# Sums rounded by one ScalarE step, statistics moved to ScalarE, and a copy moved on by one element, in a binary-convolution network

## The chip, the cores and the metric

The kernel runs on one core of a Trainium2 chip. The metric is the device time of one execution in microseconds (us). TensorE is called PE here, VectorE DVE, ScalarE ACT, GpSimd POOL, and SP is the engine that issues most DMAs.

## The reference

Four layers work on `x` of 16 images, 256 channels, 28 x 28 pixels. The change touches layers 0 and 2.

```python
# layer 0: signs convolved with signs, 3 x 3, padding 1, then a norm over batch and pixels
y  = conv3x3(sign(x), sign(w)) * mean(abs(w))      # per output channel
x  = (y - mean(y)) * rsqrt(var(y) + 1e-5) * gamma + beta + x
# layer 1: a convolution with full-precision weights on signs, a 1 x 1 one, gates
...
# layer 2: two convolutions of signs, each followed by prelu; norms before, between and after
out = sign(batchnorm(x, g1, b1))
out = prelu(conv3x3(out, sf1 * sign(w1)), a1)
out = sign(batchnorm(out, g2, b2))
out = prelu(conv3x3(out, sf2 * sign(w2)), a2)
x   = prelu(batchnorm(out, g3, b3) + x, a3)
# layer 3: attention over the 784 pixels
```

A sum over 256 channels and 9 taps of +1, -1 and 0 is a whole number of at most 2304 in size.

## The kernel before, in words

All work of one image is laid out with 128 channels on the partitions and two halves of the channels, `k` of the input and `mo` of the output. A convolution of signs (`sign_layer`) computes both output halves in one matmul: the 16-bit weight of a tap is `PACK * w[mo=1] + w[mo=0]` with `PACK = 4095`, so each PSUM value holds two whole numbers. One matmul (line L353) handles 128 input channels, one tap and half an image, 392 pixels. A **block** is half an image: 2 input halves x 3 rows of taps (`CHUNKS`) x 3 taps of a row = 18 matmuls into one PSUM bank. Layer 2 has two such convolutions of 32 blocks each (`HALVES`); layer 0 has the same 32 halves, of which the first 14 images are handled as whole images and the last half image in two quarters (`whole_images`, `PARTS`).

The moving operand comes from `fpads`, padded sign images of 30 x 30 in 16 bits for two images in turn; a tap of column `c` reads rows of 28 elements that begin `c` elements into the padded row. `sign_image(i + 1)` is issued on ACT (L466 in layer 0, L1172 in layer 2) in the first block of image `i`, ahead of that block's own eviction.

A block leaves PSUM in `apart(j)`. The value divided by `PACK` is rounded to the nearest whole number by two ACT steps: L364 adds 1.5 * 2^23 (`rounding`), L365 subtracts it (`unrounding`), which gives half 1. DVE then takes `PACK` times half 1 from the PSUM value, which gives half 0 (L367). The result lies in `ab`, in layer 2 f32 with three buffers, in layer 0 the 16-bit tile `n`, which POOL stores to `n0d` (L628) and SP loads again in layer 1 (L455).

`post(j - 1)` works on the block before. In layer 0 it takes statistics (L626, BN_STATS). In layer 2, for each half, DVE applies prelu into `p` (L1206) and takes BN_STATS of `p` (L1208); ACT squares half 0 into `doubts` (L1211), a check whether the two numbers were ever too large to be taken apart.

`Moments` keeps the statistics. Parts below `EARLY = 22` go into `parts`, and `gather` reduces them to one entry in the middle of block 23 (L169, L170); the later parts lie beside that entry in `fin`, and after the last block `mom()` reduces `fin` (L186). The next layer's scale and shift, and its first sign, wait for that: this is the seam between two convolutions. PE is kept warm over it by matmuls on zeros (`keep_busy`, L446).

PE, ACT, DVE and SP run `sign_layer` in an order written out by hand (`tc.manual_schedule`). For iteration `j` this is: the matmuls of block `j`; on a first half the sign of the next image; `post(j - 1)` on DVE; at one block `gather`; `apart(j)`; and then the squares of block `j - 1` on ACT. Three PSUM tiles (`conv_ps`) serve the blocks in turn.

SP's loads of `p` for later images of layer 2's first convolution (`load_p`, L1181) are issued within the sign of an earlier one: `load_p(i + 5)` with `sign2a(i)`. L432 are two loads of the same kind for the attention.

Layer 1 (L750) reads its middle taps, from the second image on, from `one_on`, a copy moved on by one element which SP makes (`move_on`, L724).

Of the kernel before, what the change touches and what calls it, by code (L numbers as in the profile page):

```python
# [31 lines left out]
I16 = mybir.dt.int16  # L32
# [51 lines left out]
def forward(ctx: ExitStack, tc: tile.TileContext, d: dict, out: bass.AP, careful: bool):  # L84
# [68 lines left out]
    class Moments:  # L153


        def __init__(self, name, early, late, early_count):
            self.parts = const.tile([P, 2, early, 6], F32, tag="parts", name=name + "_parts")
            self.fin = const.tile([P, 2, 3 + 6 * late], F32, name=name + "_fin")
            self.mv = const.tile([P, 2, 2], F32, name=name + "_mv")
            self.early, self.count, self.name = early, float(early_count), name  # L160

        def part(self, at, k):
            return self.parts[:, k, at, :] if at < self.early else self.fin[:, k, 6 * (at - self.early) + 3:][:, 0:6]

        def gather(self):

            nc.gpsimd.memset(self.fin[:, :, 0:1], self.count)
            for k in range(2):
                V.bn_aggr(self.fin[:, k, 1:3], self.parts[:, k].rearrange("p c s -> p (c s)"))  # L169
            V.tensor_scalar(self.fin[:, :, 2:3], self.fin[:, :, 2:3], self.count, None, ALU.mult)  # L170
# [164 lines left out]
    def sign_layer(pads, w, temp, room, sign, post, steps, moments, blocks, together=1):  # L335
# [9 lines left out]
        def products(*js):  # L345
            for j in js:
                pss[j] = conv_ps()
            for n, (k, g) in enumerate(CHUNKS):
                for j, (h, r0, rows) in ((j, p) for j in js for p in pieces(blocks[j])):
                    for t in range(3):  # L350
                        r, c = divmod(3 * g + t, 3)
                        r += r0
                        T.matmul(  # L353
                            pss[j][:, n // size if careful else h, :rows * S].rearrange("p (a b) -> p a b", b=S),
                            lhsT=w[:, n, t, :], rhs=pads[:, blocks[j][0] % 2, k, r:r + rows, c:c + S],
                            start=(n % size == 0 and t == 0), stop=(n % size == size - 1 and t == 2),
                        )

        def apart(j):
            for g in range(groups):  # L360
                n = blocks[j][2] * S
                t, ab = temp("t1")[:, :n], room(blocks[j], g)
                ps = pss[j][:, :, :HN] if blocks[j][2] == S else pss[j][:, g, :n]
                A.activation(by_halves(t, blocks[j]), ps, AF.Identity, bias=rounding, scale=1.0 / PACK)  # L364
                A.activation(ab[:, 1], t, AF.Identity, bias=unrounding)  # L365
                a, b = (by_halves(ab[:, mo], blocks[j]) for mo in range(2))
                V.scalar_tensor_tensor(a, b, -PACK, ps, ALU.mult, ALU.add)  # L367
                if g == 0:
                    abs_[j] = ab
                else:  # L370
                    tt(abs_[j], abs_[j], ab, ALU.add)

        def sign_image(i):

            for r0, r1 in ((0, HR + 1), (HR + 1, S)) if i == 0 else ((0, S),):
                sign(i, slice(r0, r1), lambda k: inner(pads[:, i % 2], k, r0, r1))
# [39 lines left out]
    def block_moments(name, blocks):  # L416
        return Moments(name, EARLY, len(blocks) - EARLY, EARLY * HN)
# [16 lines left out]
    with tc.tile_pool(name="ps_conv", bufs=3, space=PSUM) as psc, \  # L434
# [13 lines left out]
        with tc.tile_pool(name="ph1", bufs=1) as ph:  # L448
# [15 lines left out]
            def sign0(b, rows, out):  # L464
                for k in range(2):
                    A.activation(out(k), img(xs[b][:, k, :])[:, rows], AF.Sign, saturate=False)  # L466
                if rows.stop == S and b + 3 < B:
                    load_x(b + 3)
# [684 lines left out]
        with tc.tile_pool(name="ph2", bufs=1) as ph:  # L1153
# [8 lines left out]
            def room2(block, part):  # L1162
                return ph.tile([P, 2, HN], F32, tag="ab", name="ab", bufs=3)[:, :, :block[2] * S]
# [19 lines left out]
            def sign2a(i, rows, out):  # L1183
                sign2(x2[order[i]], sg1, bg1, rows, out)
                if rows.stop == S and i + 5 < B:
                    load_p(i + 5)
# [4 lines left out]
            def post2(order, alpha, mom, doubt):  # L1191
# [4 lines left out]
                def post(block, ab):  # L1196
                    i, r0, rows = block
                    for mo in range(2):
# [6 lines left out]
                        else:  # L1205
                            V.scalar_tensor_tensor(p, y, alpha[:, mo:mo + 1], y, ALU.mult, ALU.max)  # L1206
                        for h, _, m in pieces(block):
                            V.bn_stats(mom.part(first_part(block) + h, mo), p[:, h * HN:h * HN + m * S])  # L1208

                    def square(h, m):  # L1210
                        A.activation(  # L1211
                            temp("t2")[:, :m * S], ab[:, 0, h * HN:h * HN + m * S], AF.Square, scale=SAFE**-0.5,
                            accum_out=doubt[:, first_part(block) + h:first_part(block) + h + 1],
                        )

                    squares = [lambda h=h, m=m: square(h, m) for h, _, m in pieces(block) if not careful]
                    if i < B - 1:
# [13 lines left out]
            if careful:  # L1231
# [7 lines left out]
            mom = block_moments("l2b", HALVES)  # L1239
            sign_layer(fpads, w2a, temp, room2, sign2a, post2(order, pv("a1"), mom, doubts[:, 2 * NB:3 * NB]), steps, mom, HALVES)  # L1240
# [5 lines left out]
            mom = block_moments("l2c", HALVES)  # L1246
            sign_layer(
                fpads, w2b, temp, room2, lambda i, rows, out: sign2(pt[i], sg2, bg2, rows, out),
                post2(range(B), pv("a2"), mom, doubts[:, 3 * NB:4 * NB]), [], mom, HALVES,
# [606 lines left out]
```

## Time and profile before

| | |
|---|---|
| time, median of 3 runs | 956.71 us (956.46 to 960.13) |
| profiled execution | 956.87 us, of which the span from first to last instruction is 955.0 us |
| layer 0, first to last L353 | 7 to 108 us of the span |
| layer 2, first convolution | 463.8 to 561.8 us |
| layer 2, second convolution | 568.9 to 667.0 us |
| L353, one matmul as the profile shows it | 329 ns, overlapping the next |
| ACT L364, L365 on half an image | 587, 622 ns |
| DVE L367, L1206, L1208 on half an image | 547, 620, 570 ns |
| granted TensorE clock | 0.997 |

The profile is one profiled execution. Its page gives the busy time of each engine and the chain of work that ended last, followed back from the end: at each step to what released it. The chain can be had in order of time. The timeline lists instructions in order of start, with the idle time of the engine before one and what ended it in brackets; neighbours of one kind are merged (x and a count). A DMA's time to landing runs from its issue to its data's arrival.

### The profile page before, as it was taken

How to read it: one execution, taken by the hardware profiler on the slowest of the kernel's cores; microseconds unless marked ns; L12 is line 12 of the kernel's file. 1: busy time of each engine (PE TensorE's matmuls, PEld its weight loads, DVE VectorE, ACT ScalarE, POOL GpSimd, SP SyncE). 2: the span in 40 equal slices, each digit the busy share in tenths (PEclk: the TensorE clock that was granted, in tenths of full speed). 3: DMA queues.
4: the chain of work that ended last, by engine and by line, in shares of the span. 5: the costliest groups of instructions: out<-in, count | busy, mean ns of one | idle time of the engine just before them, and what ended most of it. 6: DMA issues, size and time to landing. Idle time of an engine off the chain costs nothing.

```text
span 955.0 us, 14909 instructions
## 1 busy us (share of the span) xinstructions
PE 936.3 (98%) x5602; PEld 581.9 (61%) x5608; DVE 772.2 (81%) x1424; ACT 718.9 (75%) x1204; POOL 136.2 (14%) x143
## 2 busy tenths in 40 slices
PE   7999999999999999999999999999999999999996
PEld 3555578787888888787555555555444444444442
DVE  3877898999998899977799978999656868677765
ACT  6887778888887888865788868887766666676652
POOL 2001100000000000000000000000235353434431
PEclk9999999999999999999999999999999999999998
DMA  9887534445533444411670000000142433434212
GB/s 331 277 305 263 181 120 138 167 179 202 185 138 138 156 170 162 148 71 68 250 290 1 1 1 2 1 1 1 26 77 68 98 107 83 120 74 131 68 68 106
DMA packets 35591, 118.73 MB, mean 124 GB/s; under 512 B 4451, under 2 KB 15909, under 8 KB 35509
## 3 DMA queue, kind: packets, MB, share of 16 engines
q1 hardware_dynamic: 29588, 86.33, 25.4%
q0 software_dynamic: 5632, 30.54, 11.9%
q8 instruction: 46, 0.75, 0.3%
q10 hardware_dynamic: 288, 0.80, 0.3%
q14 instruction: 37, 0.30, 0.1%
HBM read 72.67 MB, written 32.11 MB: 110 GB/s over the span
## 4 chain that ended last, share of the span: by engine, by line
PE 84%; DVE 7%; issue 3%; ACT 3%; DMA 2%; SPq 1%; POOL 0%; DVEq 0%; POOLq 0%; ACTq 0%
PE cv L750 29%; PE cv L353 21%; PE sc L1422 8%; PE av L1443 8%; PE cv L877 5%; PE mi L1399 5%; DVE p L1206 2%; PE sm L1485 2%; PE mi L1503 2%; PE sm L1443 1%; DVE ab L367 1%; DMA xs<-in_x_dram 1%; DVE l2c_fin L1208 1%; DVE l2b_fin L1208 1%; PE gate L845 1%
## 5 line engine op out<-in xcount | busy, mean ns | idle before, releaser
L353 PE MATMUL cv<-fpads,wpk 128*128 128x392 f16 (+1 forms) x1746 | 294.9, 331 | 2.7 <-DVE wpk L280 1.3
L750 PE MATMUL cv<-vs,w 128*128 128x392 f32 (+1 forms) x1296 | 272.4, 352 | 1.1 <-DVE vs L134 1.1
L353 PEld LDWEIGHTS <-wpk 128*128 128x128 f16 x1746 | 169.3, 97 | 128.9 <-issue 3.6
L750 PEld LDWEIGHTS cv<-vs,w 128*128 128x128 f32 x768 | 143.2, 190 | 6.2
L1426 ACT ACTIVATE es<-sc 128x784 f32<-128x784 f32 x112 | 87.3, 822 | 41.7 <-PE sc L1422 41.7
L750 PEld LDWEIGHTS <-w 128*128 128x128 f16 x768 | 69.4, 99 | 52.8 <-issue 9.1
L1422 PE MATMUL sc<-q,keyswa 64*128 64x392 f32 x448 | 89.9, 513 | 0.9 <-ACT es L1426 0.9
L364 ACT ACTIVATE t<-cv,rounding 128x392 f32<-128x392 f32 (+2 forms) x83 | 52.1, 628 | 38.7 <-PE cv L353 38.7
L1206 DVE SCALAR_TENSOR_TENSOR p<-ab,vec 128x392 f32<-128x392 f32 x128 | 79.2, 618 | 2.3
L1443 PE MATMUL av<-es,v 128*64 128x392 f32 x448 | 80.7, 499 | 0.0
L1436 POOL TENSOR_TENSOR sum<-sum,es 128x784 f32<-128x784 f32 x32 | 67.2, 2100 | 3.1 <-ACT es L1426 0.6
L1422 PEld LDWEIGHTS sc<-q,keyswa 64*128 64x128 f32 x448 | 38.9, 186 | 44.0 <-issue 17.1
L750 PE MATMUL cv<-one_on,w 128*128 128x392 bf16 x240 | 59.4, 329 | 0.0
L1410 DVE COPY keyswa<-mi 64x392 f32<-64x392 f32 x31 | 16.3, 565 | 53.2 <-ACT q L1406 53.2
L1443 PEld LDWEIGHTS av<-es,v 128*64 128x64 f32 x448 | 29.4, 136 | 47.4 <-issue 47.0
L905 POOL DMA_DIRECT2D x2d<-x x16 | 8.6, 537 | 345.4 <-DVE x L899 284.9
L732 ACT CAST vs<-vs 128x840 fp32r<-128x840 bf16 x63 | 54.0, 882 | 2.5 <-DVE vs L134 2.5
L877 PE MATMUL cv<-z,fw 128*128 128x392 f32 x256 | 48.9, 342 | 0.1
L367 DVE SCALAR_TENSOR_TENSOR ab<-ab,cv 128x392 f32<-128x392 f32 x64 | 35.4, 553 | 16.2 <-ACT ab L365 16.2
L877 PEld LDWEIGHTS cv<-z,fw 128*128 128x128 f32 x256 | 46.1, 188 | 1.0 <-ACT z L869 0.9
L1399 PE MATMUL mi<-p,wqk 128*128 128x392 f32 x124 | 45.1, 506 | 0.7 <-ACT p L1377 0.7
L1434 POOL TENSOR_TENSOR sum<-es 128x784 f32<-128x784 f32 x16 | 30.0, 1876 | 91.0 <-ACT es L1426 91.0
(294 smaller groups left out, 1531.1 us busy)
## 6 DMA issues: line engine op xcount, KB each, us to landing
xs<-in_x_dram SPq DMA_DIRECT2D x30, 784.0 KB, 5.4
one_on<-vs SPq DMA_DIRECT2D x60, 209.8 KB, 2.6
x2d<-x POOLq DMA_DIRECT2D x16, 784.0 KB, 3.6
out_dram<-p SPq DMA_DIRECT2D x15, 784.0 KB, 3.9
p<-x2d POOLq DMA_DIRECT2D x14, 784.0 KB, 6.9
p<-x2d SPq DMA_DIRECT2D x13, 784.0 KB, 15.5
n0d<-n POOLq DMA_DIRECT2D x16, 392.0 KB, 5.0
n<-n0d SPq DMA_DIRECT2D x16, 392.0 KB, 4.8
```

The lines of the kernel that those rows point to most:

```text
L353: T.matmul(pss[j][:, n // size if careful else h, :rows * S].rearrange("p (a b) -> p a b", b=S), lhsT=w[:, n, t, :], rhs=pads[:, blocks[j] ...
L364: A.activation(by_halves(t, blocks[j]), ps, AF.Identity, bias=rounding, scale=1.0 / PACK)
L367: V.scalar_tensor_tensor(a, b, -PACK, ps, ALU.mult, ALU.add)
L732: copy(v, w)
L750: T.matmul(ps.rearrange("p (a b) -> p a b", b=S), lhsT=w[:, k, c, u, mo * P:(mo + 1) * P], rhs=one_on[:, u, k, :, 0:S] if moved and c == 1 ...
L877: T.matmul(ps[:, h, :HN], lhsT=w[:, k, mo * P:(mo + 1) * P], rhs=z2[b][:, k, h * HN:(h + 1) * HN], start=(k + i == 0), stop=(k + i == 2),)
L1206: V.scalar_tensor_tensor(p, y, alpha[:, mo:mo + 1], y, ALU.mult, ALU.max)
L1399: T.matmul(ps[:, h, :HN], lhsT=wqk[:, k, :], rhs=x[b][:, k, h * HN:(h + 1) * HN], start=(k == 0), stop=(k == 1))
L1422: T.matmul(ps[:, h, :HN], lhsT=chunk[rows], rhs=qs[b][rows], start=True, stop=True)
L1426: A.activation(e, ps[:, :, :HN], AF.Exp, scale=0.125)
L1436: (V if late else nc.gpsimd).tensor_tensor(sums[b, late], sums[b, late], e, ALU.add)
L1443: T.matmul(ps[64 * h:64 * h + 64, :HN], lhsT=w, rhs=e[:, h, :], start=start, stop=stop)
```

## The change

In layers 0 and 2 the two rounding steps become one ACT step that writes a 16-bit integer; in layer 2 `ab` is 16-bit. In layer 2 the matmuls of an image read the middle column of taps from `shifted`, a copy of the padded signs moved on by one element, from image 4 on in the first convolution and from image 2 on in the second. SP makes the copy after the sign of the image, and these matmuls come last in their block. Loads that a sign issues come after that copy on SP. In layer 2, of the parts below 22, every second one has its statistics of half 1 taken as a sum (beside prelu, on DVE) and a sum of squares about a base (on ACT); `gather` turns these into one entry. Half 1 is handled ahead of half 0.

```diff
 class Moments:
+    self.sums = const.tile([P, 2, early // 2], F32, tag="sums", ...)
+    self.tot, self.base = ...
     def part(self, at, k):
-        return self.parts[:, k, at, :] if at < self.early else ...
+        if at >= self.early: ...
+        return self.parts[:, k, at // 2 if self.summed and k == 1 else at, :]
+    def by_sums(self, at, k):
+        return self.summed and k == 1 and at < self.early and at % 2 == 1
     def gather(self):
         nc.gpsimd.memset(self.fin[:, :, 0:1], self.count)
+        ps = [self.parts[:, k].rearrange("p c s -> p (c s)") for k in range(2)]
+        if self.summed:
+            h = self.early // 2
+            t, tot, n = self.parts[:, 1, h, :], self.tot, float(h * HN)
+            nc.gpsimd.memset(t[:, 0:1], n)
+            V.tensor_reduce(tot[:, 0:2], self.sums, AX.X, ALU.add)
+            V.tensor_scalar(t[:, 1:2], tot[:, 0:1], 1.0 / n, None, ALU.mult)
+            tt(tot[:, 2:3], t[:, 1:2], self.base, ALU.add)
+            tt(tot[:, 2:3], tot[:, 2:3], tot[:, 2:3], ALU.mult)
+            V.scalar_tensor_tensor(t[:, 2:3], tot[:, 2:3], -n, tot[:, 1:2], ALU.mult, ALU.add)
+            ps[1] = ps[1][:, 0:6 * h + 3]
         for k in range(2):
-            V.bn_aggr(self.fin[:, k, 1:3], self.parts[:, k].rearrange("p c s -> p (c s)"))
+            V.bn_aggr(self.fin[:, k, 1:3], ps[k])
 ...
 # sign_layer(..., shifted=None, direct=2): products
-            for n, (k, g) in enumerate(CHUNKS):
-                ...
-                    for t in range(3):
+            moved = shifted is not None and blocks[js[0]][0] >= direct
+            for taps in ((0, 2), (1,)) if moved else ((0, 1, 2),):
+                for n, (k, g) in enumerate(CHUNKS):
+                    ...
+                        for c in taps:
+                            src, c0 = (shifted, 0) if moved and c == 1 else (pads, c)
                             T.matmul(..., rhs=src[:, blocks[j][0] % 2, k, r:r + rows, c0:c0 + S], ...)
 # apart
-                A.activation(by_halves(t, blocks[j]), ps, AF.Identity, bias=rounding, scale=1.0 / PACK)
-                A.activation(ab[:, 1], t, AF.Identity, bias=unrounding)
+                    A.activation(by_halves(ab[:, 1], blocks[j]), ps, AF.Copy, scale=1.0 / PACK)
 # sign_image
-                sign(i, slice(r0, r1), lambda k: ...)
+                load = sign(i, slice(r0, r1), lambda k: ...)
+                if shifted is not None and i >= direct:
+                    to, of = (t[:, i % 2].rearrange("p k a b -> p (k a b)") for t in (shifted, pads))
+                    nc.sync.dma_start(out=to[:, 0:-1], in_=of[:, 1:])
+                if load:
+                    load()
 ...
 # room2
-    ph.tile([P, 2, HN], F32, tag="ab", name="ab", bufs=3)
+    ph.tile([P, 2, HN], F32 if careful else I16, tag="ab", name="ab", bufs=3)
 # post2
-                    for mo in range(2):
+                    for mo in (0, 1) if careful else (1, 0):
-                            V.scalar_tensor_tensor(p, y, alpha[:, mo:mo + 1], y, ALU.mult, ALU.max)
+                            V.scalar_tensor_tensor(p, y, alpha[:, mo:mo + 1], y, ALU.mult, ALU.max,
+                                accum_out=mom.sums[:, 0, at // 2:at // 2 + 1] if mom.by_sums(at, mo) else None)
+                        if mom.by_sums(at, mo):
+                            by_sums = p
+                            continue
                         for h, _, m in pieces(block):
                             V.bn_stats(mom.part(at + h, mo), p[:, h * HN:h * HN + m * S])
+                        if mom.summed and (at, mo) == (0, 1):
+                            V.tensor_scalar(mom.base, mom.part(0, 1)[:, 1:2], -1.0, None, ALU.mult)
+                    def square_p():
+                        A.activation(temp("t2")[:, :rows * S], by_sums, AF.Square, bias=mom.base,
+                            accum_out=mom.sums[:, 1, at // 2:at // 2 + 1])
+                    if mom.by_sums(at, 1):
+                        squares.append(square_p)
 # the two convolutions of layer 2
+    shifted = ph.tile([P, 2, 2, S + 2, S + 2], SIGNS, name="shifted")
-    sign_layer(fpads, w2a, temp, room2, sign2a, ...)
+    sign_layer(fpads, w2a, temp, room2, sign2a, ..., shifted=shifted, direct=4)
-    sign_layer(fpads, w2b, temp, room2, ...)
+    sign_layer(fpads, w2b, temp, room2, ..., shifted=shifted)
```

## The prediction

> **What bounds the kernel now.** I read the page first (busy shares, then the chain), then the chain in order of time, then the timeline at the ends of the layers that the diff touches.
>
> ```profile
> PE 936.3 (98%) x5602; PEld 581.9 (61%) x5608; DVE 772.2 (81%) x1424; ACT 718.9 (75%) x1204; POOL 136.2 (14%) x143
> PE 84%; DVE 7%; issue 3%; ACT 3%; DMA 2%; SPq 1%; POOL 0%; DVEq 0%; POOLq 0%; ACTq 0%
> ```
>
> PE carries 84% of the chain. What is taken from ACT or DVE in the middle of a layer is hidden, and only PE's own pace and the seams between layers count. For layer 2 the chain in order of time says where it leaves PE:
>
> ```profile
> 463.75 67.51 PE cv L353 x396
> ...
> 568.92 67.51 PE cv L353 x396
> ```
>
> 396 matmuls are 22 of the 32 blocks of a convolution. Over the last ten blocks the chain runs over DVE, though PE never stops (the window 463 to 562 holds all 576 matmuls in 98.05 us). The timeline there, in order of time, shows why:
>
> ```profile
> 543.28 0.54 DVE L367 SCALAR_TENSOR_TENSOR ab<-ab,cv 128x392 f32<-128x392 f32 x1
> 543.86 0.63 DVE L1206 SCALAR_TENSOR_TENSOR p<-ab,vec 128x392 f32<-128x392 f32 x1
> 544.52 0.57 DVE L1208 BATCH_NORM_STATS2 l2b_fin<-p 128x6 f32<-128x392 f32 x1
> 545.01 0.61 DVE L1206 SCALAR_TENSOR_TENSOR p<-ab,vec 128x392 f32<-128x392 f32 x1
> 545.65 0.57 DVE L1208 BATCH_NORM_STATS2 l2b_fin<-p 128x6 f32<-128x392 f32 x1
> 546.14 0.55 DVE L367 SCALAR_TENSOR_TENSOR ab<-ab,cv 128x392 f32<-128x392 f32 x1
> ...
> 561.85 0.59 ACT L364 ACTIVATE t<-cv,rounding 128x392 f32<-128x392 f32 x1 [0.22 <-PE cv L353]
> 562.47 0.62 ACT L365 ACTIVATE ab<-t,unrounding 128x392 f32<-128x392 f32 x1
> 563.29 0.55 DVE L367 SCALAR_TENSOR_TENSOR ab<-ab,cv 128x392 f32<-128x392 f32 x1
> ```
>
> A block costs DVE 2.86 us start to start and PE 3.055. `gather` (1.46 us, 538.94 to 540.40) puts DVE behind in block 23, and eight blocks at 3.055 - 2.86 win back 1.6. PE ends at T31 = 561.81; the last L367 starts 1.48 later, where ACT's two steps alone would allow about 1.28. The second convolution repeats this to 0.05 us.
>
> **PE's pace.** Read one by one in the trace, the starts of L353 in layer 2 are 166.6, 177.2 and 166.1 ns apart for taps 0, 1 and 2: the middle tap, whose rows begin one 16-bit element on, costs 11 ns more. The Trainium skill, "TensorE: Matmul & The Clock Gate", section "Wait — 56ns, not 53.3ns?", gives N/2.4 + 2.5 ns, 165.8 for N = 392: taps 0 and 2 agree, tap 1 does not, and the section has no term for it. Layer 1 already reads such a tap from a moved copy:
>
> ```profile
> 133.56 0.49 PE L750 MATMUL cv<-one_on,w 128*128 128x392 bf16 x2
> 133.89 0.83 PE L750 MATMUL cv<-vs,w 128*128 128x392 bf16 x4
> ```
>
> Two moved taps pass in 133.89 - 133.56 = 0.33 us, 165 ns each.
>
> **Part 1, middle taps from the copy.** In the first convolution images 4 to 15, in the second images 2 to 15: 26 images x 12 = 312 taps x (177.2 - 166.1) = **3.5 us** off PE, which is the path; a block falls to 2.99. Bounds: 0 if the address was not the cause, 3.9 if they reach 164.8.
>
> Added: 26 copies on SP, 450 KB each, all behind a sign. Nearest row:
>
> ```profile
> one_on<-vs SPq DMA_DIRECT2D x60, 209.8 KB, 2.6
> ```
>
> That copy is 8 packets of 71 ns per DMA engine, 0.57 us, so 2.0 is fixed; the Trainium skill, "DMA: Bandwidth & Descriptors", section "Latency and other measured facts", also names some 2 us of fixed cost. With 3598-byte rows the moving part is 1.2, so I take 3.3 us to landing; the ends are 2.6 (as the smaller one) and 5.6 (in proportion to bytes). When is it needed? With t = 0 at the end of image i-1, ACT does the eviction (0.5) and one square (0.5), then sign(i+1) for 1.96: done at 3.0. Image i+1 starts at 5.98 and, its twelve outer taps being first, reads the copy at 5.98 + 12 x 0.166 = 7.97. The copy lands at 3.1 + 3.3 = 6.4. Slack 1.6 us: I cost it at nothing. Queued behind it on SP are seven loads of p (from image 9 on), until now issued by 477, and L432's two. A p load is needed five images, 30 us, later and lands in 15.5 even in today's crowd; L432's data is read at 673. ACT's sign must now also wait until the old copy has read the pad: that was done an image earlier.
>
> **Part 2, one ScalarE step.** L365 goes (64 x 0.62 in layer 2, 19 in layer 0). What is left has no bias operand: the Trainium skill, "ScalarE: Activation LUTs", section "What ACT_TABLE_LOAD costs", prices a pointer operand at 93 ns, and the trace agrees (L364 587 against 478 for L1406's copy of that shape). I take 0.48. Inside the layers ACT had room (81 of 98 us), so nothing there. DVE stays at full-width pace: "VectorE: DVE Perf Modes", section "What auto-detection actually checks", asks for 16 bits in every tensor, and p and the PSUM sums are f32; L700 with int16 takes 1029 against 1030 for L742 without. L367 writing int16 in layer 0 suggests +15 ns.
>
> **Part 3, statistics.** Eleven BN_STATS per convolution go (0.57 each), eleven accumulator reads (about 0.08) and on ACT eleven squares (0.8) come, all in blocks below 22 where DVE has slack: nothing. `gather` grows by five dependent small operations at 0.2 (as 562.10, 562.30, 562.50 in the first seam) less 0.25 for a shorter aggregate (132 inputs 0.7, 63 inputs 0.44): 1.46 to 2.2 us. The base's one small step is in the first block, hidden.
>
> The order within a block turns: channel half 1 comes first. Today L1206 follows L367 on its own output (543.28 to 543.86, 0.58); independent neighbours start 0.49 apart (544.52 to 545.01). Half 1 needs ACT's result only, so a block should cost DVE 2.86 - 0.09 + 0.015 = 2.78.
>
> **The seams of layer 2.** L367 of block 22 starts at T22 + 0.55; one DVE block and `gather` later, at T22 + 0.55 + 2.78 + 2.2 = T23 + 2.54, that of block 23 (now T23 + 3.03). Eight blocks win back 8 x (2.99 - 2.78) = 1.7: T31 + 0.86 against 1.48. Each seam gains **0.6**, two make 1.2. If the turn saves nothing: T23 + 2.64, less 0.9 = T31 + 1.7, a loss of 0.25 each. At best L367 waits for ACT alone, T31 + 0.55: 0.9 each.
>
> **The seam of layer 0.** First a line of the timeline, then two of the chain, which there goes through the store and reload of n:
>
> ```profile
> 101.39 0.56 DVE L367 SCALAR_TENSOR_TENSOR n<-n,cv 128x392 int16<-128x392 int16 x1 [0.86 <-ACT n L365]
> ```
>
> ```profile
> 105.17 3.64 DMA n0d<-n
> 108.96 3.13 DMA n<-n0d
> ```
>
> From 101.39 to the aggregates at 109.95 DVE hardly pauses, and it began with a 0.86 wait for L365. Without it DVE starts at 100.5, the store of image 14 and the last statistics come some 0.8 earlier; SP's small loads, issued until 108.2, hold the reload at a gain of 0.75. I take **0.7** (0.2 to 0.9).
>
> **Sum.** 3.5 + 1.2 + 0.7 = 5.4. The profiled execution took 956.87 (span 955.0 and 1.87 around it), 0.16 above the median 956.71: 956.87 - 5.4 = **951.5 us**.
>
> **Rivals.** (a) *The seams of layer 2 give nothing*: turning the order saves no time (a wait on the whole of ab instead of half), `gather`'s growth eats the shorter eviction. 3.5 - 0.5 + 0.7 = 3.7: 953.2. For it: DVE has only 0.13 us of room a block then; against: the 0.49 spacing. (b) *The address is not the cause*: only the seams, 1.9 or less, 955. Against: layer 1's 165 ns. (c) *Late copies, slower*: an image can't be shorter than 3.1 + landing - 1.99 us. Up to a landing of 4.9 that is below 5.98 and free; beyond it every us costs 26 us. In proportion to bytes, 5.6, it is 0.7 x 26 = 18 lost: 970. It turns slower than before by a landing of 5.1. For it: 15.5 us landings early in the layer; against: they come from 13 loads in a row, which are through before image 4, and the fixed share above. (d) The seams at their best, 0.9 each and 0.9, with 3.9 from PE: 6.6, 950.3.
>
> **Chances.** A measurement of this kernel can tell about 0.5%, 4.8 us: faster means below 951.9. Main case 0.60, of which three quarters lies below; (a) 0.20, a fifth of it below; (b) 0.07; (c) 0.06; (d) 0.07. Faster 0.45 + 0.04 + 0.07, rounded to 0.57; slower 0.05; the same 0.38. The range 949.6 to 954.8 leaves (c), most of (b) and some of the edges out.
>
> **What would show it.** L353 starts even at 166 ns in images with a copy, blocks of 2.99; no PE idle before a middle tap (else (c)); L367 of block 31 within 0.9 us of PE's end, and L1206 0.49 after L367 (else (a)); L365 gone and L364 near 0.48; the reload of n issued before 108.3. I am wrong if middle taps stay at 177 ns, if PE waits for the copy, or if DVE's block exceeds 2.9.

## The result, and the profile after

| | before | after |
|---|---|---|
| time, median (lowest to highest) | 956.80 us of 6 runs (955.90 to 960.13) | 952.35 us of 6 runs (951.89 to 953.11) |
| ratio after to before, 95% interval | | 0.9946 (0.9931 to 0.9961) |
| profiled execution, its span | 956.87, 955.0 us | 951.89, 950.0 us |

The kernel is 0.54% faster, 952.35 against a forecast of 951.5. The median lies just above the 951.9 below which the forecast would have called the gain measurable, but the interval of the ratio leaves out 1. The sum behind the forecast was off in two places, which nearly cancel. The two profiled executions, cut at the same marks (us; a seam runs from the end of one layer's last matmul to the start of the next layer's first; the closing runs from the end of the last DVE instruction that makes the output to the end of the span):

| part | before | after | change | in the sum |
|---|---|---|---|---|
| layer 0, first to last matmul | 100.63 | 100.28 | -0.35 | 0 |
| seam after layer 0 | 6.88 | 5.98 | -0.90 | -0.7 |
| layer 1 to the first matmul of layer 2 | 349.02 | 349.03 | +0.01 | 0 |
| first convolution of layer 2 | 98.05 | 96.40 | -1.65 | -1.6 |
| seam between the convolutions | 7.11 | 6.31 | -0.80 | -0.6 |
| second convolution | 98.05 | 96.00 | -2.05 | -1.9 |
| seam to the attention | 9.14 | 8.52 | -0.62 | -0.6 |
| attention, first four matmuls | 1.52 | 1.39 | -0.13 | 0 |
| the rest of the attention | 270.66 | 270.55 | -0.11 | 0 |
| closing | 6.71 | 8.32 | **+1.61** | 0 |
| sum | 955.0 | 950.0 | -5.0 | -5.4 |

Ahead of the closing 6.6 us are gained; 1.6 are given back after the last result has been computed. The 0.35 in layer 0 lies in its first image (8.66 us before, 8.31 after, later images 6.12 in both): PE waits there for the first loads, and they landed earlier in this execution. In another execution of the same kernel layer 0 took 101.94, with a first image of 9.97. So the 0.35 is not counted for the change, which leaves 6.3.

On the page, the busy times and the shares of the chain:

```profile
PE 932.5 (98%) x5608; PEld 581.7 (61%) x5608; DVE 758.2 (80%) x1436; ACT 672.5 (71%) x1165; POOL 136.4 (14%) x145
PE 95%; DVE 1%; ACT 1%; DMA 1%; SPq 1%; issue 0%; DVEq 0%; ACTq 0%
```

PE's share of the chain rose from 84 to 95%, while its own busy time fell by only 3.8 us. In layer 2 the chain has left DVE; it now runs over PE throughout, seams included. In order of time (start, duration, what):

```profile
462.52 96.40 PE cv L376 x576
558.91 6.47 PE unused L478 x30
565.39 95.84 PE cv L376 x576
661.23 8.43 PE unused L478 x39
669.75 0.57 PE mi L1452
```

All 576 matmuls of a convolution are on it, where before the last ten blocks ran over DVE. L478 are the matmuls on zeros of `keep_busy` (L446 before), called warm-up matmuls below: in layer 2 they now end a little after what they bridge. The timeline of DVE late in the first convolution, one block from L394 (L367 before) to the next:

```profile
540.12 0.55 DVE L394 SCALAR_TENSOR_TENSOR ab<-ab,cv 128x392 int16<-128x392 int16 x1
540.59 0.62 DVE L1239 SCALAR_TENSOR_TENSOR p<-ab,vec 128x392 f32<-128x392 int16 x1
541.24 0.57 DVE L1247 BATCH_NORM_STATS2 l2b_fin<-p 128x6 f32<-128x392 f32 x1
541.73 0.61 DVE L1239 SCALAR_TENSOR_TENSOR p<-ab,vec 128x392 f32<-128x392 int16 x1
542.37 0.57 DVE L1247 BATCH_NORM_STATS2 l2b_fin<-p 128x6 f32<-128x392 f32 x1
542.86 0.55 DVE L394 SCALAR_TENSOR_TENSOR ab<-ab,cv 128x392 int16<-128x392 int16 x1
```

Start to start 2.74 us, where it was 2.86: prelu follows the subtraction by 0.47 instead of 0.58. And the end of that convolution:

```profile
557.76 1.16 PE L376 MATMUL cv<-shifted,wpk 128*128 128x392 f16 x6
...
558.95 0.50 ACT L392 ACTIVATE ab<-cv 128x392 int16<-128x392 f32 x1 [1.18 <-PE cv L376]
559.48 0.56 DVE L394 SCALAR_TENSOR_TENSOR ab<-ab,cv 128x392 int16<-128x392 int16 x1
559.96 0.62 DVE L1239 SCALAR_TENSOR_TENSOR p<-ab,vec 128x392 f32<-128x392 int16 x1
```

PE ends at 558.91. The last subtraction starts 0.57 later, right behind ACT's one step; before, it was 1.48 later and behind DVE's own backlog. The groups of the page for that ACT step, the moved taps and the copies:

```profile
L392 ACT ACTIVATE ab<-cv 128x392 int16<-128x392 f32 x64 | 31.8, 496 | 57.4 <-PE cv L376 54.5
L376 PE MATMUL cv<-shifted,wpk 128*128 128x392 f16 x312 | 60.2, 328 | 0.0
shifted<-fpads SPq DMA_DIRECT2D x26, 449.8 KB, 2.7
```

The 312 moved taps never waited for anything (last column 0.0). Read singly in the trace, nearly all start 165 to 168 ns before the next matmul, and a block of an image with a copy takes 2.985 us instead of 3.055.

### The profile page after: what moved, and what is told of

Same layout as the page of the kernel before. It is cut to its first block, busy times and chain, and to the rows that moved or that the text cites. A ratio compares the mean times of both kernels' runs of the same rounds, so it can differ in the third digit from the quotient of the medians.

```text
span 950.0 us, 14937 instructions
## 1 busy us (share of the span) xinstructions
PE 932.5 (98%) x5608; PEld 581.7 (61%) x5608; DVE 758.2 (80%) x1436; ACT 672.5 (71%) x1165; POOL 136.4 (14%) x145
## 4 chain that ended last, share of the span: by engine, by line
PE 95%; DVE 1%; ACT 1%; DMA 1%; SPq 1%; issue 0%; DVEq 0%; ACTq 0%
PE cv L376 30%; PE cv L782 29%; PE sc L1475 8%; PE av L1496 8%; PE cv L909 5%; PE mi L1452 5%; PE sm L1538 2%; PE unused L478 2%; PE mi L1556 2%; PE sm L1496 1%; DMA xs<-in_x_dram 1%; PE gate L877 1%; PE hid L685 1%; SPq L269 0%; DVE r L1522 0%
## 5 line engine op out<-in xcount | busy, mean ns | idle before, releaser
L376 PE MATMUL cv<-fpads,wpk 128*128 128x392 f16 (+1 forms) x1434 | 247.6, 329 | 1.7 <-DVE wpk L301 1.3
L1239 DVE SCALAR_TENSOR_TENSOR p<-ab,vec 128x392 f32<-128x392 int16 x128 | 77.3, 617 | 0.0
L392 ACT ACTIVATE ab<-cv 128x392 int16<-128x392 f32 x64 | 31.8, 496 | 57.4 <-PE cv L376 54.5
L1475 PEld LDWEIGHTS sc<-q,keyswa 64*128 64x128 f32 x448 | 38.9, 186 | 44.0 <-issue 17.1
L376 PE MATMUL cv<-shifted,wpk 128*128 128x392 f16 x312 | 60.2, 328 | 0.0
L394 DVE SCALAR_TENSOR_TENSOR ab<-ab,cv 128x392 int16<-128x392 int16 x64 | 35.7, 558 | 27.7 <-ACT ab L392 27.5
## 6 DMA issues: line engine op xcount, KB each, us to landing
one_on<-vs SPq DMA_DIRECT2D x60, 209.8 KB, 2.7
shifted<-fpads SPq DMA_DIRECT2D x26, 449.8 KB, 2.7
```

Of the source, the lines that this page charges most:

```text
L376: T.matmul(pss[j][:, n // size if careful else h, :rows * S].rearrange("p (a b) -> p a b", b=S), lhsT=w[:, n, c, :], rhs=src[:, blocks[j][ ...
L392: A.activation(by_halves(ab[:, 1], blocks[j]), ps, AF.Copy, scale=1.0 / PACK)
L1475: T.matmul(ps[:, h, :HN], lhsT=chunk[rows], rhs=qs[b][rows], start=True, stop=True)
```

## The experiments

The theory after this result: (1) the 11 ns of a middle tap are a matter of its address; (2) the seams of layer 2 need the turn of the halves and the one-step rounding together, and the statistics by sums (part 3) add nothing; (3) warm-up matmuls cap what the seams can give; (4) the 1.6 us of the closing come from where SP's last instructions stand in its stream, not from anything that the change computes. Rivals stand with each run.

### The address, by itself

```diff
-                            src, c0 = (shifted, 0) if moved and c == 1 else (pads, c)
+                            src, c0 = (pads, c)
```

> The kernel after, its copies still made and its middle taps still last in their block, but read from the padded rows at an address one 16-bit element on. Theory (the address costs the 11 ns): middle taps go back from 166 to 177 ns, a block of a copied image from 2.985 to 3.055 us, the first convolution of layer 2 grows by 144 x 11 ns = 1.6 us and the second by 168 x 11 = 1.9 us, 3.5 together. Rival (the order of the taps, all middle ones last, is what helps): both convolutions stay within 0.3 us of 96.40 and 96.00.

Measured (one execution, 955.51 us): 98.06 and 97.95 us, together 3.61 more than after. The chain of this kernel in order of time has the first convolution as

```profile
462.59 98.06 PE cv L376 x576
```

to the hundredth what it was before (98.05), though the taps are in the new order and the copies are made. Read singly, its middle taps take 177 to 179 ns to the next start, its other taps 165 to 168. These others read the same tile, so what slows the middle ones is not the tile but where the rows begin in it. The seams stayed at 6.31 and 8.52. So the address is the cause, and the order of the taps and the transfers cost PE nothing.

### How late may a copy be

Each copy is made twice into the same place:

```diff
-                    nc.sync.dma_start(out=to[:, 0:-1], in_=of[:, 1:])
+                    for _ in range(2):
+                        nc.sync.dma_start(out=to[:, 0:-1], in_=of[:, 1:])
```

> The kernel after with every copy of layer 2 made twice, one after the other into the same place, so that it counts as landed some 2.7 us later (effective landing 5.4 instead of 2.7). Slack by the trace of after: the copy lands 1.9 to 2.3 us before the first middle tap. Theory (slack of about 2): PE waits 0.4 to 0.8 us ahead of the first middle tap of every copied image. If only the excess counts, 26 x 0.6 = 16 us more; if the wait also delays ACT's next sign so that it feeds on itself, an image takes landing + 1.1 = 6.5 us in place of 5.97 and the loss is 26 x 0.5 = 14 us. Rival (the two copies overlap in the DMA engines and land together, or the slack is larger than read): no change in the convolutions' 96.40 and 96.00 us.

Measured: 968.22 us in one execution; the convolutions take 105.62 and 103.92, 17.1 us more than after. The chain, in order of time, leaves PE for the sign and both copies:

```profile
488.64 1.87 ACT fpads L1205 x2
490.51 0.02 issue
490.53 3.69 DMA shifted<-fpads
494.23 0.02 issue
494.24 2.96 DMA shifted<-fpads
497.20 0.04 issue
497.24 1.17 PE cv L376 x6
```

The second landed mostly 5.4 to 7.7 us after the first was issued, later than expected. Image by image the trace shows two constants. A copy is issued 3.10 us after the start of the image before (the prediction's 3.1). And a late first middle tap moves the start of the next image by as much. An image thus takes 7.12 + landing - (length of the image before); for landing 5.45 after an image of 6.14 that makes 6.43, and the trace has 6.43. With 5.97 as the least, it comes out to 0.02 in 18 of the 24 images whose landing the trace has, and to 0.22 in the others. Lateness is not paid once per image: a delay gives the next copy the same time more, so the price of a steady lateness is about half. The limit is where this gives 5.97: 7.12 + landing - 5.97 = 5.97, a landing of 4.82.

### The parts of the seams in layer 2

Five kernels vary them. Three are these edits; the other two are before and after.

Turn undone, in the kernel after:

```diff
-                    for mo in (0, 1) if careful else (1, 0):
+                    for mo in (0, 1):
```

> The kernel after with half 0 ahead of half 1 again in the statistics of layer 2. Theory (half 1 first saves DVE the wait on its own output): DVE's block goes from 2.73 to between 2.80 and 2.86 us; block 23's subtraction stays near T23 + 2.4 and eight blocks win back 8 x (2.985 - 2.82) = 1.3 in place of 1.8, so the last one starts 1.0 to 1.3 after PE's end in place of 0.57 and the two seams grow by 0.2 to 0.5 us each over 6.31 and 8.52 (the first 0.25 to 0.35 of the lag are hidden by the warm-up matmuls). Rival (the turn is nothing to DVE): block 2.73, lag 0.57, seams unchanged.

Statistics by sums undone, in the kernel after:

```diff
-            mom = block_moments("l2b", HALVES, True)
+            mom = block_moments("l2b", HALVES)
```

and the same for `"l2c"`.

> The kernel after with all statistics of layer 2 by BN_STATS again: no sums beside prelu, no squares about a base on ACT, the short gather. Theory (the statistics of the early blocks lie where DVE has room, and the last subtraction already stands at its floor): gather falls from about 1.95 to about 1.46 us, block 23's lag from 2.36 to about 1.9, block 31's stays 0.57, both convolutions and both seams stay within 0.05 us, so this part of the change is worth nothing. Rival (DVE needs the 11 statistics that were taken from it): the lags before block 22 grow above 0.6 and carry into the seam, 0.2 us or more each.

The turn alone, in the kernel before:

```diff
-                    for mo in range(2):
+                    for mo in (0, 1) if careful else (1, 0):
```

> The kernel before with the turn alone: in layer 2's statistics half 1 ahead of half 0, two rounding steps and all else as before. Theory (the turn and the one-step rounding are worth something only together): DVE's block falls from 2.86 to 2.73 us and eight blocks win back 8 x (3.055 - 2.73) = 2.6 of the lag of about 2.9, but the last subtraction then waits for ACT's two steps, T31 + 1.28 at the earliest in place of 1.48; with 0.1 more from the last block's own turn each seam falls by 0.3 us, to about 6.8 and 8.85. Rival (the turn alone is the whole gain of the seams): 6.3 and 8.5. Second rival (with f32 sums the turn saves DVE nothing): 2.86, seams 7.11 and 9.14. SP is unchanged, so its closing stays at 6.4 to 6.7.

Measured in one execution each (958.29, 954.16 and 953.03 us for the turn alone, without the turn and without the sums; all in us; lag: start of a block's subtraction after PE's end of that block, in the first convolution):

| kernel | PE block | DVE block | lag, block 23 | lag, block 31 | seams |
|---|---|---|---|---|---|
| before | 3.055 | 2.86 | 3.04 | 1.48 | 7.11, 9.14 |
| before + turn | 3.055 | 2.73 | 2.92 | 1.31 | 6.84, 9.02 |
| after - turn | 2.985 | 2.86 | 2.48 | 1.46 | 7.09, 9.04 |
| after - sums | 2.985 | 2.73 | 1.84 | 0.57 | 6.31, 8.52 |
| after | 2.985 | 2.73 | 2.36 | 0.57 | 6.31, 8.52 |

Without the turn the new kernel's seams are back where they were. Its timeline shows the old spacing of 0.58, although `ab` is 16-bit by now:

```profile
546.23 0.55 DVE L394 SCALAR_TENSOR_TENSOR ab<-ab,cv 128x392 int16<-128x392 int16 x1
546.81 0.63 DVE L1239 SCALAR_TENSOR_TENSOR p<-ab,vec 128x392 f32<-128x392 int16 x1
```

Why the one-step rounding has no visible worth there: two other parts of the change take it back. At block 22, ahead of `gather`, the lag is 0.57 instead of 1.76. Then the `gather` of the sums is 0.56 longer, so that at block 23 only 0.56 of the gain is left (3.04 to 2.48). And PE's faster pace leaves DVE only 8 x (2.985 - 2.86) = 1.0 to win back where it had 8 x (3.055 - 2.86) = 1.6. The moved copy thus raises the price of a slow DVE block. The turn alone, on the other side, runs against ACT's two steps (1.31) and gives 0.27 and 0.12. Together they reach the floor of ACT's one step. The sums cost 0.5 at block 23, and with the turn the eight blocks absorb it: in this kernel the part is worth nothing to the time.

That the turn is needed thus holds for the kernel with the sums. No run leaves out both. An estimate from the figures above: block 23 at 2.48 - 0.5 = 2.0, less 1.0 won back, ends at 1.0 in block 31 instead of before's 1.48, about half a us less lag without any turn.

The layer 0 seam of the kernel with the turn alone took 8.67 instead of 6.88. Its edit does not reach layer 0. The reload of `n` was issued at 110.13 there (108.96 before), behind a store that took 4.34 to land (3.64 before). It then took 3.91 instead of 3.13, beside the last store, which was issued at the same moment. Why the first of these stores was slower was not found out.

### The seam of layer 0, by itself

In the kernel before, for layer 0 alone:

```diff
+                if w is w0 and not careful:
+                    A.activation(by_halves(ab[:, 1], blocks[j]), ps, AF.Copy, scale=1.0 / PACK)
+                else:
                     A.activation(by_halves(t, blocks[j]), ps, AF.Identity, bias=rounding, scale=1.0 / PACK)
                     A.activation(ab[:, 1], t, AF.Identity, bias=unrounding)
```

> The kernel before with one change only: layer 0 rounds into the 16-bit integer by one ACT step; layer 2 is as before and SP has as many DMAs as before. Theory (the seam after layer 0 is a part by itself): that seam falls from 6.88 to about 6.0 us, both convolutions of layer 2 stay at 98.05 with seams of 7.11 and 9.14, and the closing stays at 6.7; the time is about 955.9. Rival (the 0.9 came from layer 0's loads or from elsewhere in the change): the seam stays within 0.2 us of 6.88.

Measured: seam 5.98, convolutions 98.06 and 98.05, seams of layer 2 7.12 and 9.13, closing 6.44, time 955.67 in one execution. The whole 0.90 is this part's. It is also steadier: with two steps the seam was 6.88, 8.67 and 6.75 in three kernels that are alike in layer 0, because the reload of `n` lands there about when the statistics are ready, and in the 8.67 it landed 1.7 us after them; with one step it was 5.98 to 6.01 in all eleven executions. The chain of after shows what comes last now, the statistics:

```profile
108.30 0.42 DVE l_fin L658 x2
108.84 0.78 DVE l_mv L207 x2
```

### Fewer warm-up matmuls

```diff
-            keep_busy(28)
+            keep_busy(25)
-            keep_busy(30)
+            keep_busy(27)
-                keep_busy(39)
+                keep_busy(35)
```

> The kernel after with fewer warm-up matmuls on zeros: 25, 27 and 35 in place of 28, 30 and 39 after layer 0 and after the two convolutions of layer 2. Theory (PE is still busy with them when the next layer's first sign is ready): the seam after layer 0 falls by up to 0.5 us, that between the convolutions by 0.2 to 0.3 us (the sign is ready at 564.96, PE starts at 565.23), that to the attention by 0.35 us (p ready at 669.30, PE starts at 669.65); about 0.6 to 1.1 in all up to the last DVE instruction. Rival (the sign's chain is the limit and the matmuls merely end with it): all three seams within 0.1 us of 5.98, 6.31 and 8.52. If the clock falls for lack of warm-up, the first blocks after a seam would grow instead.

Measured: 952.86 us (951.61 to 953.09 in 4 runs), ratio to before 0.9949 (0.9930 to 0.9967), no different from after. The seams are 5.98, 6.09 and 8.18. After layer 0 the warm-up caps nothing; in layer 2 it capped 0.22 and 0.34. But most comes back at once: the first block of the second convolution takes 3.17 instead of 3.055, the first four matmuls of the attention 1.58 instead of 1.39. The clock did not do this. The fourth matmul of the block, the first on the other input half, starts 0.29 us after the third instead of 0.17, because the sign of that half ends only then (at 566.06, the matmul starts at 566.11). The net worth of the cap is 0.10 and 0.15 us: the sign's first step sets the start, and its second one comes just behind. No run takes the warm-up matmuls away altogether, so whether the clock needs them is not shown; with these numbers of them it was granted at 0.996, as in after.

This execution also shows what the others don't. In each convolution one middle tap waited for its copy. The timeline at image 11, and the DMA view of 526 to 532:

```profile
531.36 1.16 PE L376 MATMUL cv<-shifted,wpk 128*128 128x392 f16 x6 [0.22 <-DMA shifted<-fpads]
```

```profile
q1 hardware_dynamic: 144, 0.46, 19.4%
q8 instruction: 1, 0.02, 0.9%
q14 instruction: 1, 0.01, 0.5%
...
shifted<-fpads SPq DMA_DIRECT2D x1, 449.8 KB, 5.2
```

The copy shared the DMA engines with two fetches of instructions (the kind `instruction`) and landed in 5.2 us instead of 2.7. Packet by packet the trace shows how: fifteen of the sixteen shares of the copy had arrived by 528.5, as usual; the eight packets of the last one ran from 529.17, just where the larger fetch (16 KB, 528.31 to 529.18) ends, to 530.82. PE lost 0.38 there, and 0.09 at a landing of 4.91 in the second convolution: both are the excess over the limit of 4.82, to 0.01. In the other executions with one copy an image, the copy at this place took 3.6 to 4.6 beside the same two fetches, in after 3.8, which was in time. What differs is when the larger fetch comes. Four copies of each execution meet one (images 4 and 11 of the first convolution, 5 and 12 of the second). In nine executions the trace has the landing of 35 of them, and 34 landed 2.0 to 2.1 us after the end of their fetch; the other, 1.0 after, is the 4.91, whose fetch came latest. What sets the moment of a fetch was not found out.

### The closing

26 tiny copies on SP during the attention, in the kernel after:

```diff
                 store(b - 2)
+                for _ in range(2):
+                    nc.sync.dma_start(out=spare, in_=x[b - 2][0:32, 0, 0:1])
```

> The kernel after with 26 further tiny copies on SP (128 bytes each, SBUF to SBUF) spread over images 2 to 14 of the attention; nothing is computed differently. After the last DVE instruction the kernel after takes 8.32 us to its end, the kernel before 6.71, and in the kernel after SP stands still for 2.04 us between the last two semaphore waits of its closing. Theory (SP's instructions come in by blocks, and the 26 copies of the change moved the closing over the edge of one): another 26 move the edge elsewhere, the 2 us stop goes from that place, and the closing falls to about 6.7, so that the time is about 950.7. Rival (the stop belongs to semaphore 118 or to a transfer of the data): it stays, closing 8.3 and the time 952.3. A third: it is length that counts, and more instructions on SP lengthen the closing further, above 8.3.

And in the kernel before, three of them for each of 12 images:

```diff
                 store(b - 2)
+                for _ in range(3 if b > 2 else 0):
+                    nc.sync.dma_start(out=spare, in_=x[b - 2][0:32, 0, 0:1])
```

> The kernel before with 36 tiny copies (128 bytes each) on SP spread over images 3 to 14 of the attention; nothing is computed differently. They bring SP from 373 recorded instructions to about 428, the number that the kernel after has. Theory (where the closing stands in SP's instruction stream sets whether a fetch falls into it): the closing grows from 6.71 to between 8.1 and 9.1 us, as in every kernel with 422 to 428, and the time to about 958.5. Rival (the long closing comes from something else in the change): it stays at 6.4 to 6.9 and the time at about 956.8.

Measured: after with 26 more, 950.73 us (950.33 to 951.06 in 4 runs), ratio to before 0.9931 (0.9914 to 0.9948), closing 6.88. Before with 36 more, 958.36 us, closing 8.37. **The same kind of addition made one closing 1.4 us shorter and the other 1.7 longer.** For the first kernel the whole time says so too (after took 951.37 to 954.28 in twelve runs). The second was run once, and before took 956.58 to 960.06 in the same rounds, so there only the trace can say it. The views of line L79, where SP waits in turn for eight semaphores at the end (instruction, count, shortest/median/longest in ns, first and last start), first of after, then of after with 26 copies:

```profile
L79 SPq EVENT_SEMAPHORE  x8: 17/17/17, 945.7 to 948.3; - x8
```

```profile
L79 SPq EVENT_SEMAPHORE  x8: 17/17/17, 946.2 to 946.8; - x8
```

Every wait lasts 17 ns, so none has anything to wait for. In after, the eight are spread over 2.6 us with a hole of 2.04 between the seventh and the eighth; with the padding they take 0.6. With taps from the padded rows (the same copies on SP) the hole lay further on, behind the thirteenth of these short instructions. The closing has two parts: until the first of these instructions SP stands still for 3.9 to 4.9 us in every kernel, and then comes the rest. All the kernels, by SP's recorded instructions:

| SP instructions | closing, us | of it the rest |
|---|---|---|
| 373 (three kernels) | 6.71, 6.44, 6.66 | 2.5 to 2.7 |
| 422 to 428 (seven executions of six kernels) | 8.12 to 9.13 | 3.5 to 5.0 |
| 446 to 467 (four kernels) | 6.64 to 6.95 | 2.3 to 2.7 |

The 8.37 of before with 426 lies among them, but only in part for the reason that was expected: its hole is 1.25, and 0.8 of its 1.66 is a longer first part (4.86 instead of 4.07). In after with 26 more the first part is longer too, by 0.6, and the rest 2.06 shorter, which is the hole. What decides about the hole, in all these runs, is how much stands ahead in SP's stream, and not what the kernel computes. Each tiny copy adds a DMA and one or two recorded instructions, so these runs do not tell which of the two counts. That SP stands still for a fetch of its instructions is the nearest reading: the DMA view has fetches in those microseconds. But kernels with the short closing have some there too, and the number of fetches in a trace doesn't separate the two kinds. The mechanism was only argued, not shown.

### The copy in layer 0 as well

```diff
+            moved0 = ph.tile([P, 2, 2, S + 2, S + 2], SIGNS, tag="vs", name="moved0")
-            sign_layer(fpads, w0, ..., together=2 if careful else 1)
+            sign_layer(fpads, w0, ..., together=2 if careful else 1, shifted=moved0, direct=3)
```

> The kernel after with the moved copy in layer 0 too, from image 3 on: 13 images, 156 middle taps. Theory (address alone, copies hidden): layer 0 from first to last matmul falls from 100.28 by 156 x 11 ns = 1.7 us to about 98.6. Rival (layer 0's DMA queues are full of the loads of x and of the weights, a landing there takes 4 to 8 us, and SP stands still for each sign with loads queued behind it): PE waits for copies, layer 0 grows by 1 us or more per late copy. SP has 13 more DMAs than after, so its closing may differ from 8.32 by up to 2 us either way and is to be read by itself.

Measured: 949.32 us (949.01 to 949.91 in 4 runs), ratio to before 0.9911 (0.9893 to 0.9929). Images 3 to 13 take 5.98 instead of 6.12. The landing is 3.6 to 5.5 us where the trace has it, but layer 0 leaves more time. Its sign ends earlier, so that the copy is issued 2.54 us into the image and not 3.10. And up to image 13 a block is a whole image: the middle taps come after 24 others, 3.98 us into the image and not 2.0. Image 14 is the first that is worked in halves; its copy came late, and it took 6.38. In its timeline the taps wait:

```profile
96.39 0.82 PE L376 MATMUL cv<-moved,wpk 128*128 128x392 f16 x4 [0.25 <-DMA moved<-fpads]
```

Layer 0 took 99.33, with a first image of 8.71 (8.31 after): without the first image the gain is 1.35 of the expected 1.7. SP has 446 instructions here, and the closing is 6.84. Layer 1 took 0.26 less than in after, and so it did in the version below; why is open.

### A better version

On top of the last: image 14 left out in layer 0, image 1 taken in in the second convolution, and 27 and 35 warm-up matmuls.

```diff
-            sign_layer(fpads, w0, ..., shifted=moved0, direct=3)
+            sign_layer(fpads, w0, ..., shifted=moved0, direct=(*range(3, 14), 15))
-                if shifted is not None and i >= direct:
+                if shifted is not None and i in direct:
-            keep_busy(30)
+            keep_busy(27)
-                keep_busy(39)
+                keep_busy(35)
```

> The kernel after with: a moved copy in layer 0 for images 3 to 13 and 15 (image 14 left out, for which the copy came late); from image 1 on in the second convolution of layer 2; 27 and 35 warm-up matmuls in place of 30 and 39. By the sum of what was measured: layer 0 falls by 12 images x 0.13 = 1.6 us from 100.3 to 100.6, the two seams of layer 2 by 0.26 net of the slower first blocks, the second convolution by 0.13; SP has 234 DMAs as in the kernel whose closing was 6.84, so 1.5 comes back there. 952.3 - 1.6 - 0.4 - 1.5 = 948.8. Rival: copies come late elsewhere in layer 0 now (0.3 each), or a late copy of layer 2 falls on a fetch, and it stays at 949.3 or above.

> The kernel after as it is, on the chip and in the rounds of the version above, to compare the two: 952.3, its closing between 8.1 and 9.1.

Measured: **948.95 us** (948.65 to 949.75 in 5 runs), ratio to before 0.9909 (0.9895 to 0.9924); the kernel after in the same rounds 952.66 (951.37 to 954.28 in 6 runs), 0.9945 (0.9931 to 0.9958), closing 8.94. The version's closing is 6.64, its seams 6.01, 6.09 and 8.18, layer 0 99.32 (first image 8.82). Three images of layer 0 took 6.02 to 6.04: copies that were issued up to 4.5 us into the image, or took up to 6.5 us to land in the loads' traffic, came late by some hundredths. The expectation's "100.6" is a slip: its own sum gives 98.7, and 0.6 of that gain did not come, 0.5 of it in the first image. Over the version that only adds the copy in layer 0, nothing is won that these runs can tell (948.95 against 949.32).

## Why the prediction was right, and where it was not

- **PE's pace, 3.5 us: right.** The convolutions gave 1.65 + 2.05 = 3.70. Of that 0.12 is the first block of the second one, which no longer waits at its fourth matmul. The remaining 3.58 are 312 x 11.5 ns against 11.1. By the formula in the Trainium skill, "TensorE: Matmul & The Clock Gate", section "Wait — 56ns, not 53.3ns?", 392 columns come to an estimated 165.8 ns; the moved taps' 165 to 168 agree. Rival (b) fell with the run that reads the padded rows.
- **Slack of the copies: right in kind, and thinner at its worst than the mean says.** The copy lands in 2.7 us where nothing is beside it, not 3.3. The reading behind 3.3 took the median of layer 1's copies, 2.6, for an undisturbed landing. Undisturbed ones of that group (209.8 KB) land in 2.17, of which 0.57 move bytes; the 449.8 KB move in 8 x 139 ns = 1.11. So both have the same 1.6 beside the moving, less than the 2.0 of the prediction and than the some 2 us of fixed cost that the Trainium skill names in "DMA: Bandwidth & Descriptors", "Latency and other measured facts". Slack was 1.9 us beside the loads of `p` and 2.1 later, against 1.6, but 1.0 to 1.5 for the three copies of after that a fetch delays. The limit of 4.9 was good (4.82).
- **The price in rival (c): wrong by about two.** "Beyond it every us costs 26 us" took each image to be as long as its own late copy asks. The doubled copies show that a delay gives the next copy more time. By that rule a steady landing of 5.6 would cost an estimated 26 / 2 x (5.6 - 4.82) = 10 us, not 18.
- **The ACT step, 0.48: 0.496.** 587 - 496 = 91 ns went with the bias operand, close to the 93 that the Trainium skill prices in "ScalarE: Activation LUTs", "What ACT_TABLE_LOAD costs". The function and the type of the output changed in the same step, and no run takes them apart.
- **The seams of layer 2, 0.6 each: 0.80 and 0.62.** The steps were each a little off. The turn saved 0.13 a block, not 0.09 - 0.015. `gather` grew to 2.03, not 2.2. (The small operations that the forecast names as "562.10, 562.30, 562.50" stand at 462.10 to 462.50, ahead of layer 2; the 0.2 read from them is right.) So block 23 stood at 2.36 (forecast 2.54) and block 31 reached ACT's floor of 0.57, which the forecast had only as the best case (0.86 in the main one). That is 0.91 of lag, and about 0.1 from the turn within the last block (with the turn alone, 0.17 of lag made 0.27 of seam). With fewer warm-up matmuls the seams do show that sum, 1.02 and 0.96 less than before; with all of them 0.22 and 0.34 of it are held back, of which 0.12 and 0.13 reappear in the first block and in the attention's first four matmuls. The forecast named no such cap: what came last after DVE was PE itself, with its warm-up matmuls.
- **Rival (a)** was the right question: without the turn the seams do give next to nothing, 0.02 and 0.09. Of its two mechanisms the wait on the whole of `ab` did not occur; the other, that `gather`'s growth eats the shorter eviction, is half of what the kernel without the turn shows.
- **The seam of layer 0, 0.7: 0.90.** The step that failed is "SP's small loads ... hold the reload at a gain of 0.75". SP had issued these loads by 106.1 (108.2 before), the reload went out at 106.70, 0.8 ahead of the layer's last matmul instead of 1.1 behind it, and landed at 109.79. So it is no longer the last to come: the scale and shift are ready at 110.9, the chain after goes through the statistics (L658, L207), and the full gain shows.
- **The closing, 0: +1.6.** The sum carried the end of the kernel over unchanged. Nothing in the profile of before announced this, but the 26 DMAs were counted only for what is queued behind them, not as instructions. With the closing short, the time is the 950.7 of the padded kernel: near rival (d)'s 950.3, with seams of layer 2 at ACT's floor but less of it reaching PE than (d) had.

So the parts were forecast by the right mechanisms, but that the total came so close was luck: 1.2 us more gain than forecast ahead of the closing, 0.35 of it the first loads', met 1.6 of loss in it.

## What to carry to other kernels

When a step on the critical engine gets faster, work out anew what the engines behind it can still win back before the seam: here the faster PE took from DVE the room that hid its backlog, a longer `gather` added to it, and the turn of two independent operations gave it back. Prove slack with a limit (here landing 4.8 us against 2.7), and look at what shares the transfer's path at its worst moment (5.2). And take the stretch after the last result as a part of its own when kernels a few us apart are compared: here it moved by 1.4 to 1.7 us through nothing but tiny copies on SP.

## What was not expected of the hardware

- The closing of this program takes 6.4 to 7.0 or 8.1 to 9.1 us; the long form came with 422 to 428 recorded SP instructions, the short one with 373 and with 446 to 467.
- A 16 KB fetch of instructions holds one of the sixteen shares of a 450 KB copy, and with it the copy's landing, from 2.7 up to 5.2 us: 34 of 35 such copies landed 2.0 to 2.1 us after the fetch's end.
- Twice the bytes of an SBUF copy (450 against 210 KB) took 0.54 us more to land, 2.71 against 2.17 where nothing was beside it; the median of the smaller group, 2.7, hides this, since many of its copies have other transfers beside them.
